# A one-column memset on GpSimd behind every gather of a sparse four-layer graph network

## The chip, the cores and the metric

The kernel runs on one core of one Trainium2 chip. The metric is device time in microseconds; the median of three runs of the kernel before is 1197.93 us (1197.63 to 1202.9). The core has five engines: TensorE (PE in the profile; PEld are its weight loads), VectorE (DVE), ScalarE (ACT), GpSimd (POOL) and SyncE (SP), which only issues transfers here.

## The reference

Four graph layers run one after the other on 4096 nodes with 128 features each. `adj` is a 4096 x 4096 matrix with few entries that are not zero; these are crowded into the first rows and columns, and the diagonal is full.

```python
h = relu(layernorm(x)); x = x + h @ W_self.T + (adj @ h) @ W_neigh.T + b              # layer 0
h = relu(layernorm(x)); T1 = adj @ h; T2 = 2 * (adj @ T1) - h                         # layer 1
x = x + h @ w[0] + T1 @ w[1] + T2 @ w[2] + bias
h = relu(layernorm(x)); H = h @ weight.T                                              # layer 2
C = (H @ att_src)[None, :] + (H @ att_dst)[:, None]
Tau = adj.T * exp(maximum(0.2 * C, C))
x = x + (adj.T * (Tau / Tau.sum(1, keepdims=True))) @ H
h = relu(layernorm(x)); s, d = h @ msg_w[:, :D].T, h @ msg_w[:, D:].T                 # layer 3
agg[i] = sum_j gelu(s[i] + d[j] + msg_b) * adj[i, j]
f = gelu(concat(h, agg) @ upd_w.T + upd_b) + h
x = x + layernorm(f) * ln_w + ln_b
```

## The kernel before

The nodes are reordered on the host so that nodes with many neighbours stand first. The kernel (`sparse_stack`) then works on blocks of 128 nodes and never multiplies the whole matrix. A dense version (`dense_stack`) stands behind a branch for inputs that don't fit the sparse one's fixed sizes; it isn't run here.

Layers 0 to 2 take the matrix in 16 stripes of 256 rows (`ROWS`) or columns (`COLS`). In each stripe some blocks ("near": the first ones and the stripe's own) are multiplied densely. For the rest, a list is made of the nodes that have an entry in the stripe, at most `cap` chunks of 128, and only these are fetched:

- `fetch_row` and `fetch_col` hold the numbers of the nodes, `seg_row` and `seg_col` the numbers of the pieces of the matrix that belong to them. They are worked out on the core (`row_flags`, `col_flags`, `pairs`) while the matrix is read for the first time.
- `Layer.gather` (L1102) fetches, for a chunk, the 128 rows of the layer's input from a table in DRAM (`h_tab`, `u_tab`) into one of 14 buffers `g`, and in the first pass also the 128 pieces of the matrix (`rseg`), which SP then stores in `r_tab` for the next two passes. `Layer.multiply` (L1124) consumes them on TensorE: L1138 the dense blocks, L1155 the fetched chunks.
- `fetch_columns` (L731) fetches the pieces of columns (`cseg`) that the attention of layer 2 needs, and SP stores them in `c_tab`. `Attention.rows` (L1208) fetches rows of `a_tab` into `g`; `attend` uses them on ScalarE (L1228) and TensorE (L1252, L1254).

Layer 3 works on single entries. `scan` and `entries` find them; `values` (L930) fetches the value of 128 entries at a time (`e_val`), and `Messages.rows` (L1344) fetches the 128 rows of `d_tab` that belong to them into `m`, or into halves of the former buffers `e` and `tau` (the profile then names these). TensorE adds the row of the other node (L1406, L1408), ScalarE takes the gelu (L1412), TensorE sums (L1418).

All these fetches go through one helper, `gather`, at L552: an indirect transfer that GpSimd issues[...]. The profile puts all of them on L553. Beside them GpSimd does little: constants at the start, twelve additions of a bias (L979, L1000), four memsets (L1592).

The order of the instructions on each engine is fixed when the kernel is built. `Plan` (L255) runs all parts as generators; each names an engine and a supposed duration before it issues, and the plan always takes the one that could begin first, with a rank among those that begin at about the same time. A gather is planned with `GATHER = "POOL", 1.27` (L376). `in_order` (L348) then fixes the order for every engine. What the engines wait for is set by semaphores.

Where the plan sees a gap on TensorE, `fill` (L604) puts matmuls of zeros (L609) into a free bank of `banks` or `picks`.

Of the kernel before, what the change touches and what calls it, by code (L numbers as in the profile page):

```python
# [27 lines left out]
P = 128  # L28
# [350 lines left out]
def sparse_stack(tc, x, adj, adjT, diag, w_self, w_neigh, b0, w1, b1, w2, att_src, att_dst,  # L379
# [7 lines left out]
    nc = tc.nc  # L387
    plan = Plan()
    EARLY = 7
    with ExitStack() as ctx:  # L390
# [4 lines left out]
        def tiles(pool, name, n, shape, dtype=F32):  # L395
            return Slots([pool.tile(list(shape), dtype, name=f"{name}{i}", tag=f"{name}{i}") for i in range(n)])

        def kept(name, shape, dtype=F32):
            return keep.tile(list(shape), dtype, name=name, tag=name)
# [17 lines left out]
        banks = tiles(ps, "bank", 3, (P, BANK))  # L417
        picks = tiles(ps, "pick", 2, (P, BANK))
# [130 lines left out]
        junks = tiles(keep, "junk", 2, (P, D))  # L549
        aggs = tiles(keep, "agg", 2, (P, BANK))  # L550

        def gather(dst, table, index):  # L552
            nc.gpsimd.indirect_dma_start(out=dst, out_offset=None, in_=table[:, :],  # L553
                                         in_offset=bass.IndirectOffsetOnAxis(ap=index, axis=0))


        def norm(blocks, dst):
# [45 lines left out]

        def fill(begin, time):  # L604

            idle = min((free, i, slots.items) for slots in (banks, picks) for free, i in slots.free + [(1e9, 0)])
            if idle[0] < begin - 1.0:
                for _ in range(int(time / 0.22)):
                    nc.tensor.matmul(idle[2][idle[1]], nothing[:, :P], nothing, start=True, stop=True)  # L609
# [121 lines left out]
        def fetch_columns():  # L731
            for s in COLS:
                if s.cap:
                    yield col_list[s.index]
                for k in range(s.cap):
                    t = yield csegs
                    yield GATHER
                    gather(t, adj_segments, seg_col[:, s.chunk + k:s.chunk + k + 1])
                    here, left = Event(), Count(1)
                    here.set(plan.transfer(P * CS * 4))  # L740
                    plan.start(store(here, t, csegs, left, c_tab[s.index][k * P:(k + 1) * P, :], c_done[s.index],
                                     P * CS * 4), 6)
                    plan.start(give_back(left, csegs, t), 0)
# [186 lines left out]
        def values():  # L930
            for number, group in enumerate(GROUPS):
                yield decoded[number]
                for u in group.units:
                    for k in range(u.chunk, u.chunk + u.cap):
                        yield GATHER
                        n = u.within(k)
                        gather(e_val[:n, k:k + 1], adj_flat, e_at[:n, k:k + 1])
                        valued[u.number].set(plan.finish + plan.LANDING)
                    plan.start(valid(u), 7)
# [125 lines left out]
        class Layer:  # L1065
# [36 lines left out]
            def gather(self):  # L1102
                for s in ROWS:
                    if s.cap:
                        yield row_list[s.index]
                    for c in range(s.cap):
                        if self.number == 0:
                            t = yield rsegs
                            yield GATHER
                            gather(t, adjT_segments, seg_row[:, s.chunk + c:s.chunk + c + 1])  # L1110
                            here, left = Event(), Count(2)
                            here.set(plan.transfer(P * RS * 4))
                            self.at["seg", s.index, c] = t, here, left
                            plan.start(store(here, t, rsegs, left, r_tab[s.index][c * P:(c + 1) * P, :],
                                             r_done[s.index], P * RS * 4), 2)
                            plan.start(give_back(left, rsegs, t), 0)
                        g = yield rows_g
                        yield self.table_done
                        yield GATHER
                        gather(g[:, :D], self.table, fetch_row[:, s.chunk + c:s.chunk + c + 1])  # L1120
                        self.at["row", s.index, c] = g
                        self.rows_here[s.index][c].set(plan.transfer(P * D * 4))
# [528 lines left out]
def gnn_stack_kernel(tc, **args):  # L1651


    some_bad = sparse_stack(tc, **args)
    with tc.If(some_bad > 0):
        args.pop("diag")
        dense_stack(tc, **args)
# [329 lines left out]
```

## Time and profile before

| | |
|---|---|
| median of three runs | 1197.93 us |
| the profiled execution | 1500.43 us |
| its span, first to last instruction | 1498.6 us |
| mean granted TensorE clock | 0.834 |
| GpSimd busy | 767.3 us, 832 instructions |
| of it gathers (L553) | 736, together 728.4 us |
| bytes read and written in HBM | 203.41 MB, 31.23 MB |

The profiled execution is 302.5 us longer than the median of the runs. Its times are good for what follows what and for the duration of single instructions; the length of its stages must not be carried over.

In a row of the groups, the first part is line, engine, operation and what it writes from what; after the bar stand the busy time, the mean of one instruction and the idle time of that engine just before, with what ended it. In the chain of waits, "issue" and "another core or an unknown queue" are time for which no wait that the profile knows is responsible. The gathers by what they fetch:

| fetched | number | mean us of one |
|---|---|---|
| `e_val` from `adj` | 158 | 0.984 |
| `g` from `h_tab`, two passes | 136 | 0.998 |
| `g` from `a_tab` | 74 | 1.049 |
| `cseg` | 74 | 0.957 |
| `rseg` | 68 | 1.048 |
| `g` from `u_tab` | 68 | 0.951 |
| rows of `d_tab` (`m`, `tau`, `e`) | 70, 63, 25 | 0.972, 0.961, 0.970 |

### The profile page before, as it was taken

Reading aid. Unit: us, or ns where it says so; the run is one execution under the profiler, and the core shown is the slowest. Engines: PE = TensorE matmul, PEld = TensorE weight load, DVE = VectorE, ACT = ScalarE, POOL = GpSimd, SP = SyncE. Lnnn points to the kernel's source line nnn. Section 1 sums busy time; section 2 is a strip of 40 time slices with the busy share of each in tenths; the row PEclk is TensorE's granted clock in tenths of the full one; section 3 lists DMA queues with packets and bytes.
Section 4 is the critical chain, followed back from the end, with each engine's and each line's share of the span. In section 5 each row is a group of like instructions: output and inputs, shape, how many; then the busy total and the mean of one; then the engine's idle time right before and its main releaser. Section 6 shows DMA issues by size and latency. Waiting matters only on the chain.

```text
span 1498.6 us, 19187 instructions
## 1 busy us (share of the span) xinstructions
PE 1058.5 (71%) x5943; PEld 723.0 (48%) x5943; DVE 791.5 (53%) x2982; ACT 670.3 (45%) x1344; POOL 767.3 (51%) x832
## 2 busy tenths in 40 slices
PE   6786788887477867467774289668777955668880
PEld 3454555554256556355653255334444633556660
DVE  5796666886366566355663156334343612344453
ACT  5983666663121212114452087546564801236462
POOL 4135754544455656635667527726576165654500
PEclk9897898888697888677897599879897986888885
DMA  8999999994366778666542045313333121121200
GB/s 252 352 338 318 335 308 342 341 310 145 92 194 191 205 217 232 171 193 176 156 132 80 22 123 146 108 39 87 107 101 97 41 59 43 47 51 48 67 17 17
DMA packets 175415, 236.03 MB, mean 157 GB/s; under 512 B 22452, under 2 KB 155336, under 8 KB 167112
## 3 DMA queue, kind: packets, MB, share of 16 engines
q1 hardware_dynamic: 148904, 186.45, 37.6%
q0 software_dynamic: 26400, 48.27, 13.1%
q8 instruction: 49, 0.80, 0.2%
q14 instruction: 62, 0.51, 0.1%
HBM read 203.41 MB, written 31.23 MB: 157 GB/s over the span
## 4 chain that ended last, share of the span: by engine, by line
PE 26%; issue 11%; ACT 9%; another core or an unknown queue 8%; DVE 5%; DMA 1%; SPq 0%; ACTq 0%; DVEq 0%
PE acc L1254 4%; PE acc L1252 4%; PE bank L597 3%; PE acc L1138 3%; PE acc L1155 2%; PE acc L1418 2%; PE pick L609 1%; PE bank L1406 1%; PE bank L1408 1%; ACT e L1228 1%; ACT junk L1450 1%; ACT e L1231 1%; ACT junk L568 1%; PE pick L1418 1%
## 5 line engine op out<-in xcount | busy, mean ns | idle before, releaser
L553 POOL DMA_INDIRECT e_val<-in_adj,e_at x158 | 155.5, 984 | 48.0 <-issue 46.5
L553 POOL DMA_INDIRECT g<-h_tab,fetch_row x136 | 135.7, 998 | 73.1 <-issue 34.3
L609 PE MATMUL pick<-nothing 128*128 128x512 f16 x532 | 141.4, 413 | 2.4 <-issue 2.4
L1138 PE MATMUL acc<-big,hA 128*128 128x256 f32 x448 | 124.6, 422 | 16.3 <-DMA big<-in_adjT 7.3
L609 PEld LDWEIGHTS <-nothing 128*128 128x128 f16 x795 | 83.5, 108 | 102.7 <-issue 38.3
L553 POOL DMA_INDIRECT g<-a_tab,fetch_col x74 | 77.7, 1049 | 92.5 <-issue 43.6
L553 POOL DMA_INDIRECT rseg<-in_adjT,seg_row x68 | 71.3, 1048 | 94.3 <-issue 39.7
L1138 PEld LDWEIGHTS acc<-big,hA 128*128 128x128 f32 x448 | 90.6, 213 | 32.8 <-DMA big<-in_adjT 8.8
L553 POOL DMA_INDIRECT cseg<-in_adj,seg_col x74 | 70.8, 957 | 66.2 <-DVE pcum L634 23.5
L553 POOL DMA_INDIRECT g<-u_tab,fetch_row x68 | 64.7, 951 | 63.7 <-PE acc L1155 32.5
L890 DVE SCALAR_TENSOR_TENSOR ehit<-ehit,pos,pick 128x32 f32<-128x32 f32 (+7 forms) x158 | 38.8, 285 | 108.0 <-issue 64.6
L1235 DVE TENSOR_TENSOR tau<-e,big 128x512 f32<-128x512 f32 (+3 forms) x61 | 54.2, 889 | 70.2 <-ACT e L1231 43.7
L887 ACT COPY ehit<-pick 128x192 f32<-128x192 f32 (+7 forms) x74 | 20.4, 286 | 157.8 <-remote 72.5
L553 POOL DMA_INDIRECT tau<-d_tab,e_col x63 | 60.5, 961 | 56.2 <-PE acc L1418 15.1
L553 POOL DMA_INDIRECT m<-d_tab,e_col x70 | 68.0, 972 | 38.0 <-issue 16.5
L768 ACT ACTIVATE mask<-dst 128x2048 fp8e4<-128x2048 f32 x43 | 81.8, 1903 | 12.1 <-DMA dst<-in_adj 9.5
L1155 PE MATMUL acc<-big,g 128*128 128x256 f32 x272 | 80.8, 437 | 2.7 <-DMA big<-r_tab 1.9
L622 ACT ACTIVATE sel_t<-iota_row,mids 128x512 f32<-128x512 f32 (+3 forms) x43 | 27.1, 642 | 118.1 <-DVE mids L617 69.8
L568 ACT ACTIVATE junk<-xN,stat 128x128 f32<-128x128 f32 x128 | 51.4, 401 | 60.7 <-DVE stat L564 23.1
L609 PE MATMUL bank<-nothing 128*128 128x512 f16 x263 | 74.8, 430 | 1.6 <-DVE s L1369 1.2
L883 PE MATMUL pick<-eA,esel 128*128 128x65 f16 (+7 forms) x158 | 27.3, 249 | 61.4 <-DVE esel L624 24.1
L1138 PE MATMUL acc<-big,hB 128*128 128x256 f32 x224 | 64.2, 428 | 0.0
(328 smaller groups left out, 2727.5 us busy)
## 6 DMA issues: line engine op xcount, KB each, us to landing
dst<-in_adj SPq DMA_DIRECT2D x43, 1024.0 KB
big<-in_adjT SPq DMA_DIRECT2D x45, 512.0 KB
raw<-in_adj SPq DMA_DIRECT2D x21, 1024.0 KB
big<-in_adjT SPq DMA_DIRECT2D x66, 256.0 KB
big<-r_tab SPq DMA_DIRECT2D x30, 512.0 KB
c_tab<-cseg SPq DMA_DIRECT2D x74, 128.0 KB
r_tab<-rseg SPq DMA_DIRECT2D x68, 128.0 KB
big<-c_tab SPq DMA_DIRECT2D x15, 512.0 KB
```

The costliest lines, as they stand in the source:

```text
L553: nc.gpsimd.indirect_dma_start(out=dst, out_offset=None, in_=table[:, :], in_offset=bass.IndirectOffsetOnAxis(ap=index, axis=0))
L568: nc.scalar.activation(junk, src[:, k, :], AF.Square, bias=st[:, 0, k:k + 1], accum_out=st[:, 1, k:k + 1])
L597: nc.tensor.matmul(p[:, k * D:(k + 1) * D], lhs[:, k * P:(k + 1) * P], w, start=i == 0, stop=i == len(terms) - 1)
L609: nc.tensor.matmul(idle[2][idle[1]], nothing[:, :P], nothing, start=True, stop=True)
L768: nc.scalar.activation(mask[:, h * HALF:(h + 1) * HALF], raw_of[b, h], AF.Sigmoid, scale=1e38, accum_out=marks[:, 2 * b + h:2 * b + h + 1] ...
L890: nc.vector.scalar_tensor_tensor(hit[:, q, :], hit[:, q, :], pos0[:, k + q:k + q + 1], pv[:, q, W:2 * W], op0=ALU.is_le, op1=ALU.mult, acc ...
L1138: nc.tensor.matmul(acc, self.near[:, b, :D], as_rows(t)[:, k, :], start=count == 0, stop=count == every - 1)
L1155: nc.tensor.matmul(acc, row[:, :D], r, start=count == 0, stop=count == every - 1)
L1235: nc.vector.tensor_mul(tau[:, :n, :], e[:, :n, :], a[:, :n, :])
L1252: nc.tensor.matmul(acc[0:1, CS:2 * CS], parts[k][:, D + 1:], tau[:, k, :], start=False, stop=False)
L1254: nc.tensor.matmul(acc[:, :CS], parts[k][:, :D], e[:, k, :], start=False, stop=self.count[s.index] == every - 1)
L1418: nc.tensor.matmul(acc[:, b % GB * P:(b % GB + 1) * P], m[:, q, :], r[:, q, :], start=False, stop=all(self.left[g * GB + k] == 0 for k in ...
```

## The change

A tile `spacer` of 128 x 1 is added to those that are kept through the whole kernel, and `gather` writes zeros into it on GpSimd behind each indirect transfer. Nothing reads it. The supposed duration `GATHER` of the plan stays. In `fill`, the search for the idle bank compares only the time and the number of the slot, and no longer, where these are equal, the lists of tiles.

```diff
@@ -549,9 +549,13 @@
         junks = tiles(keep, "junk", 2, (P, D))
         aggs = tiles(keep, "agg", 2, (P, BANK))
 
+        spacer = kept("spacer", (P, 1))
+
         def gather(dst, table, index):
+
             nc.gpsimd.indirect_dma_start(out=dst, out_offset=None, in_=table[:, :],
                                          in_offset=bass.IndirectOffsetOnAxis(ap=index, axis=0))
+            nc.gpsimd.memset(spacer, 0.0)
 
 
         def norm(blocks, dst):
@@ -603,7 +607,8 @@
 
         def fill(begin, time):
 
-            idle = min((free, i, slots.items) for slots in (banks, picks) for free, i in slots.free + [(1e9, 0)])
+            idle = min(((free, i, slots.items) for slots in (banks, picks) for free, i in slots.free + [(1e9, 0)]),
+                       key=lambda slot: slot[:2])
             if idle[0] < begin - 1.0:
                 for _ in range(int(time / 0.22)):
                     nc.tensor.matmul(idle[2][idle[1]], nothing[:, :P], nothing, start=True, stop=True)
```

## The prediction

> **What bounds the kernel now.** I read the head of the page first (span, busy times), then the chain of waits, then the groups of GpSimd (POOL), then the gathers by stage, and last single stretches of the timeline.
>
> ```profile
> span 1498.6 us, 19187 instructions
> PE 1058.5 (71%) x5943; PEld 723.0 (48%) x5943; DVE 791.5 (53%) x2982; ACT 670.3 (45%) x1344; POOL 767.3 (51%) x832
> ...
> PE 26%; issue 11%; ACT 9%; another core or an unknown queue 8%; DVE 5%; DMA 1%; SPq 0%; ACTq 0%; DVEq 0%
> ```
>
> No engine is full, and POOL is not on the chain at all. But 19% of the chain's span, 0.19 x 1498.6 = 285 us, is time that the profile cannot put down to anything ("issue", "unknown queue"). The profiled execution took 1500.43 us (1.8 us outside its span), the median of the runs is 1197.93 us: 302.5 us less. The two numbers are so close that I take these stalls for a property of the profiled execution, mostly absent from the others. One of them, from the timeline:
>
> ```profile
> 1219.88 1.91 PE L1408 MATMUL bank<-s,msel 128*128 128x128 f32 x8
> ...
> 1253.00 0.60 ACT L1412 ACTIVATE tau<-bank 128x512 f32<-128x512 f32 x1 [35.24 <-remote]
> ```
>
> ScalarE stands for 35 us before it reads a PSUM bank whose last matmul ended at 1221.8, 31 us earlier. So POOL's share must be read against the shorter time. The gathers by stage (stretch, its length, POOL busy with gathers and their number, granted clock, DMA share, GB/s):
>
> ```profile
> 84.00:395.00 311.00, 157.10 (x153) 0.84 0.86 294
> 395.00:600.00 205.00, 108.15 (x113) 0.84 0.66 192
> 600.00:870.00 270.00, 158.45 (x168) 0.77 0.47 136
> 870.00:1185.00 315.00, 168.70 (x163) 0.89 0.33 94
> 1185.00:1430.00 245.00, 136.06 (x141) 0.83 0.20 50
> ```
>
> 736 gathers (two stand across an edge and are counted twice). The first stage runs at 86% DMA share: the adjacency is being read, and transfers bound it. After 395 us the DMA share falls, and 583 gathers remain. How they follow each other (start, duration, then the idle time of POOL before it):
>
> ```profile
> 329.25 0.94 POOL L553 DMA_INDIRECT g<-h_tab,fetch_row  x1 [0.30 <-issue]
> 330.20 1.28 POOL L1000 TENSOR_TENSOR xN<-xN,b_sb 128x512 f32<-128x512 f32 x1
> 331.64 0.97 POOL L553 DMA_INDIRECT rseg<-in_adjT,seg_row  x1 [0.16 <-PE bank L588]
> 332.91 0.94 POOL L553 DMA_INDIRECT g<-h_tab,fetch_row  x1 [0.30 <-issue]
> ```
>
> Gather behind gather: 0.30 us idle and 0.95 busy, a pitch of 1.25 us. Behind an addition the idle time is 0.16 only, and the addition itself starts with none.
>
> From the timeline I counted, stage by stage, the gathers behind another with a gap under 0.35 us: 128, 95, 148, 154, 121. After 395 us these are 518 x 0.30 = 155 us of gaps, with 571 us of gathers (the last four rows) 727 us of the 1035 us between 395 and 1430. POOL's real idle time there is 308 us. Take 285 to 302 us of stalls out of the execution, and POOL would have 6 to 23 us left, less than the waits at turns of the work that it has anyway (23.5, 26.0, 26.9 and 12.5 us in POOL's list of waits, the longest single ones of cseg, g, e and tau). It cannot all hold at once, but it says that without the stalls POOL is nearly full after the first stage: what is added to each gather is mostly paid.
>
> **What the Trainium skill says.** "Perfetto Trace Analysis", section GPSIMD Engine Instruction: an instruction that reads no tensor has no reported start, and GpSimd work is better timed by start-to-start spacing than by its reported duration. The trace agrees: memsets reported at 0.10 us start 0.02 to 0.05 us apart (below). "GPSIMD Engine Reference", section Instruction dispatch: each instruction costs a dispatch of tens of cycles on the GpSimd cores, and a following instruction is held back by nothing but its own core's work and its waits; no run here separates the cores. "SBUF — State Buffer", section Who interferes with whom: GpSimd and VectorE share one port pair under an exclusive lock, so a memset may wait for a VectorE instruction. In the trace 91 of 736 gathers take over 1.0 us instead of 0.946, 32 us in all, so such collisions may be there.
>
> **The change part by part.** It adds 736 memsets of 128x1, one behind every gather, on POOL. In the instruction lists of the two programs every other engine has the same instructions in the same order, and so have SP's and POOL's DMA queues; POOL's list differs by the 736 memsets. The key added to the search for an idle bank picks the same bank everywhere, so it costs nothing; there is nothing that it could uncover. No operation is removed or moved.
>
> The memset waits for one thing, a semaphore of POOL itself (the memset before it, over a gather earlier, 1.25 us ago), so it never waits long. Behind it stands the next gather, and behind that all later ones and the bias additions; whoever waits for gathered rows (TensorE at L1155, L1254, L1406, ScalarE at L1228, the stores of segments on SP) waits for these.
>
> Its price. The trace of before has memsets of this size at the start only:
>
> ```profile
> 0.24 0.10 POOL L1975 MEMSET const-float32-0.0<- 128x1 f32 x1 [0.24 <-issue]
> 0.28 0.10 POOL L1975 MEMSET const-float32-1.0<- 128x1 f32 x1
> 0.30 0.11 POOL L1975 MEMSET const-bfloat16-1.0<- 128x1 bf16 x1
> 0.33 0.12 POOL L1975 MEMSET const-uint8-127<- 128x1 uint8 x1
> ...
> 1.40 0.10 POOL L448 MEMSET ones<- 128x1 fp8e4 x1
> 1.44 0.09 POOL L450 MEMSET eps<- 128x1 f32 x1
> 1.49 1.01 POOL L460 IOTA hT<- 128x1024 int32 x1
> ```
>
> Reported 0.10 us; spacing 0.04, 0.02, 0.03, 0.04, 0.05 us, mean 0.036. Three readings of what one adds to the pitch of 1.25:
> - 0.036 us: the cores do the memset in that time and then need the same 0.30 us ahead of a gather. The 0.16 behind an addition is then the same 0.30, counted from a reported end that comes 0.14 later than the core was free. I take this one, because one rule then explains both gaps.
> - 0.30 is replaced by 0.10 + 0.15: minus 0.05 us, if the gap behind other work is truly shorter. The only memset before a gather shows 0.15:
>
> ```profile
> 861.98 0.53 POOL L1592 MEMSET m<- 128x512 f32 x1 [10.13 <-DVE dcol L923]
> 862.66 0.96 POOL L553 DMA_INDIRECT e_val<-in_adj,e_at  x1 [0.15 <-issue]
> ```
>
> - 0.10 us or a little more: the whole reported duration, if nothing of it lies in the gap, or if the memset meets the port lock.
>
> Sum for the first: 583 x 0.036 = 21 us of POOL work after 395 us. Of this I take three quarters as paid (between a half, because POOL still waits for buffers that TensorE frees: 32.5 us for L1155 in the third stage, and all): 16 us. The first stage's 153 x 0.036 = 5.5 us is hidden beside the adjacency's transfers (86% DMA share) and beside POOL's own waits of some 108 us there; without that cover it would be 5.5 us more. So 1197.93 + 16 = 1214 us. In the profiled execution the stalls may cover the same work: there I expect anything from 1500 to about 1530 us.
>
> **The rivals.**
> - Faster (the other side): the gap shortens. If a gather starts 0.15 us behind a memset's end and the memset is over 0.10 us behind the gather, the pitch is 1.20 us, 583 x 0.05 x 0.75 = 22 us less: 1176 us. It decides as soon as gap plus memset is under 0.30 us. For it: all six gathers that follow an addition or a memset without another wait start 0.14 to 0.16 us behind it. Against it: behind the addition the saving is 0.11 us at most (gather end to gather end 330.19 to 332.61 is 2.42, less 1.25, is 1.17 for an addition of 1.28), about what the end of an instruction is reported late.
> - No change: what delays the next gather runs from the last gather's end, 0.30 us whatever is between, and a memset of 0.04 to 0.10 us fits in it. Or POOL has slack in the runs as it has in the profile (308 us after 395). Then the memset does not do what it could either way: 1198 us. For it: gaps of 0.30 to 0.31 behind gathers of 0.92 as of 1.95 us, so the gap hangs on the end. Against it: the shorter gap behind other work.
> - Much slower: 0.10 us for each, 583 x 0.10 x 0.75 = 44 us: 1242 us; with every gather paid, 736 x 0.10 = 74 us: 1272 us. For it: the port lock, and additions of 1.54 us beside the usual 1.27. Against it: spacing of 0.036.
>
> **How the numbers follow.** 0.36 for the first reading (1214; its own range 1206 to 1227 by half to all paid and 0.03 to 0.05 us each), 0.34 for faster, 0.18 for no change, 0.12 for much slower. About 0.5% (6 us) is what a measurement of this kernel can tell from no change. Some of the first case falls within that: faster 0.34, same 0.20, slower 0.46. The range reaches below the faster case's 1176 and up to the much slower one's 1242: 1173 to 1243, which leaves out the half-and-more of the extreme cases, some 2 in 10.
>
> **What would show it.** In the changed kernel's timeline: the start-to-start time of two gathers with a memset between. 1.28 to 1.30 us supports the forecast, 1.20 the faster rival, 1.25 no change, 1.35 the much slower one. POOL's idle time before the rows that now wait on "PE acc L1155" and "PE acc L1418" should shrink by what the memsets take, and TensorE and ScalarE should show waits for gathered rows that they hardly have now (3.2 us for DMA g at L1155). A pitch that moves while the time does not would show that the slack estimate is wrong; a time that moves without the pitch would show that the memset acts on something that I have not seen, such as the unexplained stalls.

## The result, and the profile after

| | us, median (lowest to highest) | runs |
|---|---|---|
| before | 1197.21 (1190.38 to 1202.9) | 13 |
| after | 1200.68 (1191.19 to 1205.07) | 13 |

The ratio after to before is 1.0026, 95% interval 1.0004 to 1.0047. That is 3 us, below the 0.5% that the prediction set as what can be told from no change. It is in the range of 1173 to 1243 us, but that range was made wide enough for the rivals; the forecast of 1214 us was a loss of 16 us, and that did not come. All ratios here are those on record; they are not exactly the quotients of the medians.

The profiled execution of before, at 1500 us, is not like the others, and one of the chips used ran every kernel, the one before included (1549.68 us median), at such times; four of the experiments below were measured there. The comparison here is therefore with a second profile of the kernel before, the first experiment ("plain": 1198.45 us); the changed kernel's own profiled execution took 1191.19 us.

The head of the page and the chain of waits, first plain, then after:

```profile
span 1196.7 us, 19187 instructions
PE 985.6 (82%) x5943; PEld 677.3 (57%) x5943; DVE 796.7 (67%) x2982; ACT 672.9 (56%) x1344; POOL 770.5 (64%) x832
...
DMA 29%; PE 21%; DVE 15%; ACT 13%; POOL 11%; issue 9%; SPq 0%; POOLq 0%; DVEq 0%; ACTq 0%
```

```profile
span 1189.2 us, 19919 instructions
PE 979.7 (82%) x5943; PEld 670.7 (56%) x5943; DVE 793.2 (67%) x2982; ACT 672.4 (57%) x1344; POOL 862.7 (73%) x1568
...
POOL 26%; PE 22%; DMA 21%; ACT 11%; DVE 11%; issue 7%; SPq 0%; POOLq 0%; DVEq 0%; ACTq 0%
...
L558 POOL MEMSET spacer<- 128x1 f32 x736 | 95.2, 129 | 0.2
```

POOL is busy for 92 us more, and its share of the chain rises from 11% to 26%; the span does not grow. (The 7 us between the two spans say nothing: the profiled execution of after was the fastest of its 13.) The "unknown queue" of the profile before has gone from both. I read busy time and chain share as labels here: a part of the gap before a gather now carries the name of a memset. Whether time was added shows only in the distance between gathers. The timeline of POOL, first plain, then after (start, duration, idle time before it):

```profile
700.35 0.94 POOL L553 DMA_INDIRECT e_val<-in_adj,e_at  x1 [0.31 <-issue]
701.60 0.94 POOL L553 DMA_INDIRECT e_val<-in_adj,e_at  x1 [0.30 <-issue]
702.84 0.94 POOL L553 DMA_INDIRECT e_val<-in_adj,e_at  x1 [0.30 <-issue]
```

```profile
311.77 0.95 POOL L556 DMA_INDIRECT rseg<-in_adjT,seg_row  x1 [0.19 <-issue]
312.71 0.11 POOL L558 MEMSET spacer<- 128x1 f32 x1
313.02 0.94 POOL L556 DMA_INDIRECT g<-h_tab,fetch_row  x1 [0.19 <-issue]
313.96 0.12 POOL L558 MEMSET spacer<- 128x1 f32 x1
314.27 0.94 POOL L556 DMA_INDIRECT rseg<-in_adjT,seg_row  x1 [0.19 <-issue]
```

Before: 0.30 us from the end of a gather to the next start. After: 0.11 us of memset and 0.19 us idle, again 0.30. The pitch (start to start) is 1.25 us in both. Over the whole execution the median from the end of a gather to the next start is 0.305 us in both; 703 of plain's 735 gaps and 698 of after's lie under 0.33 us. The stages (stretch, length, POOL's gathers alone with their number, clock, DMA share, GB/s), plain and then after:

```profile
84.00:400.00 316.00, 178.48 (x178) 0.91 0.92 322
400.00:600.00 200.00, 145.85 (x153) 0.91 0.83 248
600.00:870.00 270.00, 206.03 (x205) 0.96 0.49 134
870.00:1145.00 275.00, 201.72 (x203) 0.96 0.32 79
```

```profile
84.00:400.00 316.00, 183.21 (x180) 0.90 0.91 322
400.00:600.00 200.00, 146.21 (x154) 0.94 0.84 250
600.00:870.00 270.00, 204.01 (x204) 0.96 0.46 130
870.00:1145.00 275.00, 198.66 (x200) 0.98 0.31 78
```

The numbers of gathers in each stretch agree within three. From 400 us on, both kernels issue a gather every 1.33 us on the average (in plain 558 in 742 us). In after's timeline the gaps above 0.6 us sum up to 24 us from there to the last gather at 1138.6; in plain's they sum up to 21. So POOL is full in both: it hardly waits for anything but its own gap. In the list of waits of plain (sum us, times, longest), engines that consume the rows stand waiting for them, which the 1500-us profile does not show:

```profile
ACT e L1228 <- DMA g<-a_tab,fetch_col: 44.9, 22, 10.9
PE acc L1155 <- DMA g<-h_tab,fetch_row: 23.6, 17, 3.5
```

So a full POOL got 736 more instructions and lost almost nothing.

### The profile page after: what moved, and what is told of

Same layout as the page of the kernel before. It is cut to its first block, busy times and chain, and to the rows that moved or that the text cites. A ratio compares the mean times of both kernels' runs of the same rounds, so it can differ in the third digit from the quotient of the medians.

```text
span 1189.2 us, 19919 instructions
## 1 busy us (share of the span) xinstructions
PE 979.7 (82%) x5943; PEld 670.7 (56%) x5943; DVE 793.2 (67%) x2982; ACT 672.4 (57%) x1344; POOL 862.7 (73%) x1568
## 4 chain that ended last, share of the span: by engine, by line
POOL 26%; PE 22%; DMA 21%; ACT 11%; DVE 11%; issue 7%; SPq 0%; POOLq 0%; DVEq 0%; ACTq 0%
POOL g L556 7%; DMA g<-h_tab,fetch_row 6%; POOL e_val L556 5%; POOL m L556 3%; PE acc L1143 3%; POOL spacer L558 3%; PE acc L1160 3%; DMA cseg<-in_adj,seg_col 3%; POOL tau L556 3%; ACT mask L773 2%; PE bank L601 2%; DMA g<-a_tab,fetch_col 2%; PE pick L614 2%; ACT junk L572 2%; DMA big<-r_tab 2%
## 5 line engine op out<-in xcount | busy, mean ns | idle before, releaser
L614 PE MATMUL pick<-nothing 128*128 128x512 f16 x532 | 138.2, 408 | 0.0
L1143 PE MATMUL acc<-big,hA 128*128 128x256 f32 x448 | 118.3, 410 | 8.9 <-DMA big<-in_adjT 8.6
L1143 PEld LDWEIGHTS acc<-big,hA 128*128 128x128 f32 x448 | 88.0, 206 | 22.7 <-DMA big<-in_adjT 9.7
L558 POOL MEMSET spacer<- 128x1 f32 x736 | 95.2, 129 | 0.2
L1160 PE MATMUL acc<-big,g 128*128 128x256 f32 x272 | 76.7, 417 | 10.6 <-DMA big<-r_tab 7.9
L1143 PE MATMUL acc<-big,hB 128*128 128x256 f32 x224 | 58.3, 395 | 14.0 <-DMA big<-in_adjT 14.0
L614 PE MATMUL bank<-nothing 128*128 128x512 f16 x263 | 69.4, 408 | 0.0
L1160 PEld LDWEIGHTS acc<-big,g 128*128 128x128 f32 x272 | 52.5, 206 | 22.1 <-issue 9.3
```

Of the source, the lines that this page charges most:

```text
L558: nc.gpsimd.memset(spacer, 0.0)
L1143: nc.tensor.matmul(acc, self.near[:, b, :D], as_rows(t)[:, k, :], start=count == 0, stop=count == every - 1)
L1160: nc.tensor.matmul(acc, row[:, :D], r, start=count == 0, stop=count == every - 1)
```

## The experiments

Two theories. **Floor**: the next gather starts at the earliest 0.30 us behind the end of the last and 0.15 us behind the end of what POOL does between; work that fits in is free, and what exceeds it is paid at every gather. **Slack**: POOL has time to spare, and the memsets use that. A third, **price**: each memset costs something beside the pitch.

**The kernel before, once more** ("plain", no edit).

> The kernel before, unchanged, profiled once more. If the profiled execution of 1500 us was a single disturbed one: a profiled time of 1190 to 1205 us, gathers 1.25 us apart with hardly a gap over 0.35 us after 400 us, and no time without a named cause of over 10 us on ScalarE. If the kernel without memsets stalls ScalarE and VectorE whenever it is profiled, and the memsets cure this: about 1500 us again, with 15 to 25% of the chain of waits under 'issue' and 'unknown queue'.

1198.45 us (a single execution) with the lines above. No stalls, gathers 1.25 us apart, POOL full. This speaks against slack before anything is changed.

**Wider memsets.** The same instruction takes longer when the tile has more columns:

```diff
-        spacer = kept("spacer", (P, 1))
+        spacer = kept("spacer", (P, 128))     # and 256, 32, 64
```

> The memset writes 128 columns. Floor theory (the next gather starts at the later of 0.30 us behind the end of the last gather and 0.15 us behind the end of what stands between): the memset ends 0.22 us behind the gather, the gap becomes 0.37, the pitch 1.32 us; with GpSimd full after 400 us (551 gathers) or throughout (736), 0.07 us each is 36 to 50 us: ratio 1.03 to 1.04. Slack theory (GpSimd has room in ordinary runs, so the one-column memset cost nothing for that reason): the pitch grows the same but the ratio stays within 1.005.

> The memset writes 256 columns. Floor theory: it ends 0.33 us behind the gather, gap 0.48, pitch 1.43 us; 0.18 us for 551 to 736 gathers is 99 to 132 us: ratio 1.08 to 1.11. Slack theory: ratio under 1.03, since the first 50 us or so are absorbed. If the time follows the pitch, the rise from 128 to 256 columns gives the share of gathers that is paid.

Measured 1252.97 us, ratio 1.0459 (1.0393 to 1.0525), and 1332.89 us, 1.1147 (1.1083 to 1.1211), against 1194.01. In the timelines of 128 and of 256 columns:

```profile
700.39 0.96 POOL L556 DMA_INDIRECT g<-u_tab,fetch_row  x1 [0.16 <-issue]
701.33 0.23 POOL L558 MEMSET spacer<- 128x128 f32 x1
701.73 0.95 POOL L556 DMA_INDIRECT e_val<-in_adj,e_at  x1 [0.16 <-issue]
```

```profile
702.88 0.33 POOL L558 MEMSET spacer<- 128x256 f32 x1
703.37 0.95 POOL L556 DMA_INDIRECT e_val<-in_adj,e_at  x1 [0.16 <-issue]
704.32 0.33 POOL L558 MEMSET spacer<- 128x256 f32 x1
704.80 0.95 POOL L556 DMA_INDIRECT e_val<-in_adj,e_at  x1 [0.16 <-issue]
```

Now the memset reaches past the floor, and the gather follows its end by 0.16 us. The gaps have a median of 0.381 and 0.488 us, 0.076 and 0.183 above plain. The ratios are 55 and 137 us, or 0.075 and 0.186 us for each of 736 gathers, both a little above the band of the floor theory. Slack is refuted: what lengthens the pitch is paid. The profiles show where. From the 179th gather to the last, plain takes 741.7 us, after 741.5, 128 columns 786.3 and 256 columns 853.2; 557 longer gaps make 42 and 102 us of the 45 and 112 (with 256 columns the gathers themselves take 10 us longer there, cause not known). From the first gather to the 179th the profiles show 335.5 and 344.8 us, against 315 to 326 in plain, in after and in other kernels with gaps of 0.305 us: 10 to 20 and 19 to 30 us, where 178 longer gaps are 14 and 33. The DMA share there is 92% in plain and 89% with 256 columns.

A rival is TensorE: its mean granted clock is 0.924 in plain and 0.904 and 0.888 here. But POOL hardly waits longer, for TensorE or for anything else: from 400 us on, its gaps above 0.6 us sum up to 23 and 27 us, against 21 in plain.

**Four memsets into the one tile.**

```diff
-            nc.gpsimd.memset(spacer, 0.0)
+            for _ in range(4):
+                nc.gpsimd.memset(spacer, 0.0)
```

> Four one-column memsets behind each gather. Floor theory with the spacing of memsets at the start of the trace (0.036 us): the last ends 0.11 + 3 x 0.036 = 0.22 us behind the gather, gap 0.37, pitch 1.32: ratio 1.03 to 1.04. If each costs its reported 0.11 us, because the core must acknowledge one before the next: 0.44 + 0.15, gap 0.59, pitch 1.54: ratio 1.13 to 1.18. Slack theory: within 1.005.

1689.09 us, 1.4128 (1.4054 to 1.4202), by far beyond what either theory gave. The timeline:

```profile
700.11 0.94 POOL L556 DMA_INDIRECT cseg<-in_adj,seg_col  x1 [0.62 <-issue]
701.05 0.59 POOL L559 MEMSET spacer<- 128x1 f32 x4
701.78 0.93 POOL L556 DMA_INDIRECT e_val<-in_adj,e_at  x1
702.71 0.58 POOL L559 MEMSET spacer<- 128x1 f32 x4
703.93 0.96 POOL L556 DMA_INDIRECT cseg<-in_adj,seg_col  x1 [0.63 <-issue]
```

Two things: the four stand 0.156 us apart (median), as each writes what the one just before wrote and waits for its semaphore; and most gathers then start 0.6 us behind the last memset (gap 1.2 us), while nearly all of `e_val` start 0.147 us behind it (gap 0.73). What tells the two groups apart in the trace is a separate semaphore wait: an instruction of POOL of its own that stands ahead of some gathers. Of 434 gathers with one behind the gather before, 422 start 0.69 to 0.74 us behind its end; the 291 without one start 0.147 us behind the last memset (median). In plain, too, of 25 gathers with such a wait just ahead and a gap over 0.5 us, 17 start 0.70 to 0.73 us behind it. What fills the 0.70 us is not shown. For the cost as a whole I had two explanations, the number of instructions and the wait for the instruction just before. The next run separates them.

**Four memsets into four tiles**, so that each waits only on the memset of the gather before:

```diff
-        spacer = kept("spacer", (P, 1))
+        spacers = [kept(f"spacer{i}", (P, 1)) for i in range(4)]
...
-            nc.gpsimd.memset(spacer, 0.0)
+            for spacer in spacers:
+                nc.gpsimd.memset(spacer, 0.0)
```

> Four one-column memsets behind each gather, each into its own tile, so that each waits for the memset of its tile one gather earlier and not for the one just before it. If the 0.67 us that four memsets into one tile cost came from waiting for each other's acknowledgement (which also keeps the sequencer from preparing the next gather): the last ends 0.11 + 3 x 0.036 = 0.22 us behind the gather, gap 0.37, pitch 1.32 us, and as with 128 columns 50 to 60 us more: ratio 1.04 to 1.05. If four instructions cost this by their number: ratio 1.35 to 1.45 again.

> The memset writes 32 columns. Floor theory: it ends 0.14 us behind the gather, plus 0.155 is 0.29, still under 0.30: pitch 1.25 us, ratio 0.997 to 1.006 as with one column. If the time grows from the first column on with the memset's length (0.0009 us a column and gather, 736 gathers): 20 us more, ratio 1.017.

> The memset writes 64 columns. Floor theory: it ends 0.165 to 0.17 us behind the gather, gap 0.32, pitch 1.27 us: 0.02 x 736 is 15 us, ratio 1.008 to 1.016. If the time grows from the first column on: 0.055 x 736 is 40 us, ratio 1.034.

> The changed kernel once more, to see whether the 1.0026 is more than the spread. Floor theory: pitch equal to 1.25 us within 0.005, ratio 0.998 to 1.004. If the memset has a small cost of its own (port collisions, longer gathers): ratio 1.002 to 1.005 with an interval above 1.

These four were measured beside a kernel before of 1549.68 us. Ratios there: four tiles 0.9763 (0.9647 to 0.9879), 32 columns 0.9999 (0.9961 to 1.0036), 64 columns 1.0033 (0.999 to 1.0077), the changed kernel 1.0141 (1.0067 to 1.0216). They do not follow the pitch, and I draw nothing from them: there stalls as in the 1500-us profile stand in the way. The gaps in their traces could be read: 0.305 us for one and for 32 columns, 0.325 for 64, 0.350 for four tiles. The times had to be measured again, beside a kernel before of 1195.46 us.

> Four memsets of one column, into four tiles, behind each of the 736 gathers, for a time on a chip where the kernel before takes about 1197 us. The traces gave a pitch of 1.295 us between gathers for this form against 1.25. If the gap behind a gather has a floor of 0.30 us that all POOL work up to it is free in, and what exceeds it is paid at every gather: 736 x 0.045 = 33 us, a ratio of 1.025 to 1.03. If it is the number of instructions that costs, as it did with four memsets into one tile (0.67 us per gather): 1.35 to 1.45. If POOL has slack behind its gathers after all: below 1.01.

> A memset of 64 columns, whose gap was 0.32 us in the trace. The floor theory: 736 x 0.02 = 15 us, a ratio of 1.008 to 1.016. If the cost grew with the width from the first column on, along the line from nothing to 128 columns (1.046), it would be half of that, 1.023 or more.

> The changed kernel again. The floor theory: the memset of one column ends inside the 0.30 us, the pitch is 1.25 us, the ratio between 0.998 and 1.004. If each memset costs something of its own after all, the ratio is 1.002 to 1.005 with an interval above 1; the forecast's 0.036 us for each of 736 would be 1.022.

Measured: four tiles 1220.3 us, 1.0209 (1.0176 to 1.0241); 64 columns 1212.77, 1.0154 (1.0113 to 1.0195); the changed kernel 1201.15, 1.0045 (1.0029 to 1.0062). Timelines of four tiles and of 64 columns:

```profile
700.12 0.20 POOL L559 MEMSET spacer<- 128x1 f32 x4
700.48 0.95 POOL L556 DMA_INDIRECT e_val<-in_adj,e_at  x1 [0.15 <-issue]
```

```profile
700.60 0.17 POOL L558 MEMSET spacer<- 128x64 f32 x1
700.93 1.04 POOL L556 DMA_INDIRECT e_val<-in_adj,e_at  x1 [0.16 <-issue]
```

Four independent memsets take 0.20 us together, 0.028 us apart. The number of instructions is cheap; it was writing the same tile, and the waits that this brings, that cost 0.67 us per gather in the run before (0.4128 x 1194.01 us over 736). The separate semaphore waits stand in this trace as well, but 370 of 381 gathers behind one start within 0.2 us of the last memset, so here they delay a gather only together with memsets that wait. The sizes came near the floor theory's: 64 columns inside its band (18 us; 15 by a gap of 0.325 against 0.305), four tiles below it (25 us; 33 by a gap of 0.350 at 736 gathers, but 25 at the 557 after the first stage, whose own 318.1 us are within the 315 to 326 of other kernels), one column just above (5 us; 0 by the pitch). For one column the outcome written down beside the floor, a small cost of its own with a ratio of 1.002 to 1.005, is the one that came; the forecast's 0.036 us for each would have been 1.022.

**What the 3 to 5 us are.** Three kernels: the tile without the memsets (one memset ahead of everything; the changed line in `fill` is in it too), two memsets into two tiles, and memsets behind the gathers after the first 200 only.

```diff
# alloc_only
         spacer = kept("spacer", (P, 1))
+        nc.gpsimd.memset(spacer, 0.0)
...
-            nc.gpsimd.memset(spacer, 0.0)
# two_tiles: as above, range(2)
# late_only
+            issued[0] += 1
+            if issued[0] > 200:
+                nc.gpsimd.memset(spacer, 0.0)
```

> The changed kernel with its tile, but one memset ahead of everything in place of the 736 behind the gathers. If the 1.0045 of the changed kernel comes from the memsets: 0.998 to 1.002 here. If it comes from the place that the tile takes, or the plan's changed line in fill: 1.003 to 1.006.

> Two memsets of one column, into two tiles, behind each gather. They take about 0.15 us by the spacing of four (0.05 us) and the one (0.11 us), so the floor theory has the gap at 0.30 to 0.31 us and the pitch at 1.25. If each memset has a small price of its own beside the pitch, the changed kernel's 0.0045 doubles: 1.008 to 1.011. If what is left is not a price per memset: 1.002 to 1.006, as with one.

> Memsets only behind the gathers after the first 200, which are 536 of 736. If the 5 us are spread evenly: 1.003 to 1.0035. If they arise in the first stage, where gathers wait for other things: 0.999 to 1.0015. If they arise only later: 1.004 to 1.006.

Against 1196.55 us: the tile alone 0.9991 (0.9961 to 1.0021), two memsets 1.0035 (1.0013 to 1.0056), late memsets 1.0020 (1.0 to 1.004). In the timeline of two tiles:

```profile
702.26 0.14 POOL L559 MEMSET spacer<- 128x1 f32 x2
702.56 0.95 POOL L556 DMA_INDIRECT e_val<-in_adj,e_at  x1 [0.16 <-issue]
```

Two memsets end 0.14 us behind the gather, and the next one still starts at 0.30. Twice as many do not cost twice as much (1.008 is outside the interval), so the remainder is not a price per memset. Without memsets nothing is seen of it, so it is probably neither the tile's place nor the line in `fill`, though the intervals of the tile alone and of two memsets touch. Late memsets could cost anything between none and nearly all of it; that run decides nothing.

**Taking work off POOL.** If POOL is full, less work on it should gain. In off_pool the eight bias additions of L1000 (1.28 us each) and four small memsets go to VectorE, planned there; in same_plan only the additions move, and the plan's cost stays, so that the other engines' order stays too:

```diff
# off_pool
-            yield "POOL", 1.4
-            nc.gpsimd.tensor_add(rows, rows, by_block(b1_sb, GB))
+            yield on_dve(BANK)
+            nc.vector.tensor_add(rows, rows, by_block(b1_sb, GB))
...
-            nc.gpsimd.memset(m, 0.0)
+            nc.vector.memset(m, 0.0)
# same_plan
-            nc.gpsimd.tensor_add(rows, rows, by_block(b1_sb, GB))
+            nc.vector.tensor_add(rows, rows, by_block(b1_sb, GB))
```

> The kernel before with the eight bias additions of L1000 and the four memsets of L1592 moved from GpSimd to VectorE, and no memset behind the gathers. It takes about 8 x 1.17 + 2 = 11 us from POOL. If POOL's work is paid in full, here as at the gathers: a ratio of 0.990 to 0.997. If those additions lie where POOL waits anyway, or VectorE is late in their place: 0.998 or more.

> The kernel before with the eight bias additions of L1000 on VectorE in place of GpSimd and the plan's cost left as it was, so that the order of the other instructions stays. It takes 8 x 1.28 = 10 us from between the gathers of the first stage and gives VectorE 8 x 0.68 us. If POOL's work is paid in full there too: 0.991 to 0.996. If the first stage has slack, or VectorE's delay takes its place: 0.998 to 1.004. If those additions on VectorE cost what off_pool cost: 1.011 or more.

off_pool: 1214.2 us, 1.014 (1.0109 to 1.017). It is no test of POOL: the plan answered the changed cost with another order on every engine. The page shows it in TensorE's count, 39 more matmuls of zeros than the 5943 of before:

```profile
PE 997.8 (83%) x5982; PEld 678.8 (56%) x5982; DVE 792.0 (66%) x2994; ACT 673.3 (56%) x1344; POOL 762.3 (63%) x820
```

same_plan: 1193.21 us, 0.9979 (0.9961 to 0.9996), 2.5 us less of the 10 that POOL no longer works. It is the one version with an interval below 1 beside a kernel before of normal times, by less than the 0.5% bound. It lies just under the second of its theories (0.998 to 1.004), and its interval reaches into that one and not into the first. The additions stand in the first stage (154 to 367 us in plain), where POOL also waits for 90 us in gaps over 0.6 us, so they may be paid only in part. Which of the waits takes the rest is open.

## Why the prediction was wrong

- **"0.036 us: the cores do the memset in that time and then need the same 0.30 us ahead of a gather."** This is the step that failed, the price of a memset in the sum. Measured: 0.00 us on the pitch. The 0.30 us run from the end of the last gather, beside the memset, and are not a preparation that begins when POOL is free. The second gap that the prediction tried to explain, 0.16 us behind an addition, is a condition of its own: 0.15 to 0.16 us behind the end of the memset or addition that stands between. The later of the two sets the start (medians in us from the traces; 32 columns from the chip with the long times):

| behind each gather | memset's end, from the gather's end | + 0.155 (second condition) | gap measured |
|---|---|---|---|
| nothing | | | 0.305 |
| 1 column | 0.114 | 0.269 | 0.305 |
| 32 columns | 0.139 | 0.294 | 0.305 |
| 2 tiles of 1 | 0.143 | 0.298 | 0.305 |
| 64 columns | 0.166 | 0.321 | 0.325 |
| 4 tiles of 1 | 0.199 | 0.354 | 0.350 |
| 128 columns | 0.220 | 0.375 | 0.381 |
| 256 columns | 0.327 | 0.482 | 0.488 |
| 4 into one tile, gathers without a separate semaphore wait | 0.582 | 0.737 | 0.728 |

  The kink is where the memset ends at 0.15 us. The other gathers of the last form start later (gap 1.2 us), so the two conditions are not the only ones. The prediction had both numbers, 0.30 and 0.15, and looked for one rule behind them where there are two.
- **The rival "no change"** had the right mechanism in its first half, with a chance of 0.18 and 1198 us. Its second half, slack on POOL, is refuted by the wide memsets. Its evidence against, "the shorter gap behind other work", is the second condition of the table.
- **The faster rival** took the 0.15 as replacing the 0.30. It does not: the shorter gap appears only where the other condition has already passed.
- **The much slower rival** counted the reported 0.10 us on top. The reported time is right (0.11), and lies inside the gap.
- **"Without the stalls POOL is nearly full after the first stage", with 6 to 23 us left**: right. plain and after show 21 and 24 us of larger gaps, and the chain of both is free of the unknown queue.
- **"Of this I take three quarters as paid", and the first stage hidden**: without weight for this change, as the price was 0. The other kernels show how it would have gone. After the 179th gather a longer pitch is paid in full (four tiles 24 us longer than plain there, 128 columns 45, where the gaps give 25 and 42), so three quarters was too low. The cover of the first stage may have held for four tiles (25 us in all); for the wide memsets it mostly failed.
- **"Profiled execution anything from 1500 to about 1530"**: missed, 1191.19 us. The stalls were rightly called a property of that execution, and then carried over to the next one.
- **The reading list held**: 1.25 us between gathers was named as the mark of no change, and it is what the trace shows. "A time that moves without the pitch" was named too; it did move by 3 to 5 us. That remainder does not double with two memsets. Its cause is open, and so is what makes the 0.30 us.
- The Trainium skill, "Perfetto Trace Analysis", section GPSIMD Engine Instruction, advises spacing over reported duration. For the price of one memset among others that holds: four start 0.028 us apart, each reported at 0.11. The prediction misapplied it: the spacing of memsets among themselves is not the price of one between gathers; the spacing of gathers shows that. The same section says that an instruction which reads no tensor has no reported start; the traces give the memsets, whose rows show no input, a start and a length, and with 128 and 256 columns the next gather follows the reported end by 0.16 us. "SBUF — State Buffer", section Who interferes with whom, left room for a port lock. For one column the gathers show no sign of it: 732.1 us in all in plain and 733.1 in after. With 256 columns they take 746.1 us; whether that is the lock is not shown.

## What to carry to other kernels

Before pricing an instruction on a full engine, find what the idle time beside it is counted from: if it runs from the end of the last long instruction, a short one between can be free up to that time and is paid beyond it, and a few runs with the instruction widened find the edge. An engine can be full while its busy share is 64% and its share of the chain of waits 11%; the pitch of its repeated instruction tells more. When the profiled execution is far from the median, have it taken again before any slack is read from it.

## What was not expected of the hardware

- A fixed 0.30 us behind the end of a GpSimd gather, in which up to 0.15 us of other GpSimd work is free.
- Four memsets that each wait on the one just before cost 0.67 us per gather; four that don't, 0.034 us (25 us over 736). With the waiting ones, a gather behind a separate semaphore wait starts 0.70 us (median) behind that wait.
- On one chip the same kernel took 1549.68 us instead of about 1196, and a kernel with more POOL work ran 2.4% shorter than the one before there. No run explains it.
